# Attention probabilities: the fourth head of each group turned by VectorE and DMAs instead of TensorE

## The chip, the cores and the metric

One core of a Trainium2 chip. The time is device microseconds of one execution; lower is better. "Span" is the time from the first to the last instruction of one profiled execution.

## The reference

Two layers over x of 8 batches x 512 tokens x 512 features, in float32. The first is a graph attention in which each of 16 heads looks at 20 tokens, in two directions. The second, which the change touches, is a conditioned self-attention:

```python
h   = gamma(w) * layernorm(x) + beta(w)          # gamma, beta from the condition, per batch
q, k, v = split(h @ Wqkv.T + bqkv)               # 16 heads of 32
att = softmax(q @ k.T) / sqrt(512)               # [512 x 512] per batch and head
out = (att @ v).reshape(512, 512) @ Wp.T + bp
h1  = out + x
x   = gamma(w) * layernorm(h1) + beta(w) + h1
```

## The kernel before, in words

The first layer fills the first 400 us of the profile and leaves its result in DRAM (`mid`). The second layer is a loop over 128 **steps** (L1060 and after), in an order written out by hand for every engine. A step is one batch `b`, one group `g` of four heads and one block `c` of 128 queries; a batch has 16 steps, numbered by `at`. In the last batch the order of groups and blocks is exchanged.

In step n the kernel does, on TensorE in this order: the scores of step n+1 (four heads, each on its own 32 rows of the array, into two PSUM tiles of two banks); in steps 1 to 4 a **turn**, four transposes of the next batch's normalized tokens; in even steps the product of the probabilities with the values for the two steps before (`weigh`, L953), each head on its own 32 columns of the array, 16 products of 128 columns per step; then the transposes of this step's probabilities, head by head (`turn_probs`, L946, four 128x128 transposes a head), with a **job** after the second head and another after the third. A transposed head goes from PSUM to SBUF by a copy on ScalarE, that of the fourth head (outside the last batch) by VectorE. A float32 product is issued as two matmuls.

VectorE takes the maxima of the scores (`tops`, L931), ScalarE the exponentials with their sums (`exps`, L936), VectorE the reciprocals and GpSimd the scaling (`normalize`, L944), all one step ahead. When a group's four blocks are done, ScalarE adds the value bias and moves the group from PSUM to `AO` (`outputs`, L984).

The jobs of a batch are 32 slots, two per step (`JOBS`): the projections q, k, v of the next batch and the output projection. Both are made of seven products of half size, from sums and differences of quarters. For the output projection GpSimd makes those of the heads' outputs (`output_sums`, L775, at the steps of `OUTPUT_SUMS_AT`), and products 1, 6 and 7 are added to the residual by GpSimd (`add_gathered`, L823, at the end of the step that made them). Jobs `("output", 1, i)` are those of the batch before, `late` ones belong to the batch itself. Four more blocks of finishing per batch (`FINISH`: statistics, norm on VectorE, L879 and L880, sums on GpSimd, L883 and L884, a store) run in steps 5 to 8. Jobs and transposes share three PSUM banks.

All loads and stores of this layer are issued on SyncE's queue. `XQ[b]` holds a batch's input: fetched once, two batches ahead, normalized, and kept until it becomes the residual.

Of the kernel before, what the change touches and what calls it, by code (L numbers as in the profile page):

```python
# [9 lines left out]
F32 = mybir.dt.float32  # L10
BF16 = mybir.dt.bfloat16
I32 = mybir.dt.int32
AF = mybir.ActivationFunctionType
# [31 lines left out]
def graph_then_self_attention(ctx: ExitStack, tc: tile.TileContext, x, x_t, near, near_t, labels, w_self_t, wq, wk_t,  # L45
# [3 lines left out]
    def blocks(ap):  # L49
        return ap.rearrange("(c p) f -> p c f", p=P)  # L50
# [37 lines left out]
    XQ, Z, HT, Q, K, V, AO, GATE, STATS, PAIRS = {}, {}, {}, {}, {}, {}, {}, {}, {}, {}  # L88
# [11 lines left out]
    def fetch(b):  # L100
        XQ[b] = xp.tile([P, C, F], F32, tag="x", name=f"xq_{b}")
        nc.sync.dma_start(XQ[b], blocks(mid[b]))

    def norm_stats(b, c, src=None):
        statistics((src or XQ[b])[:, c, :], f"{b}_{c}")

    def norm(b, c, src=None):
        if c == 0:
            Z[b] = turned.tile([P, C, F], F32, tag="turned", name=f"z_{b}")
        mv = STATS[f"{b}_{c}"]  # L110
        nc.vector.tensor_scalar(Z[b][:, c, :], (src or XQ[b])[:, c, :], mv[:, 0:1], mv[:, 1:2], ALU.subtract, ALU.mult)
# [62 lines left out]
    with ExitStack() as l0:  # L174
# [452 lines left out]
        for n, (b, c) in enumerate(slots):  # L627
# [77 lines left out]
            if n in (23, 28):  # L705
                fetch((n - 23) // 5)
# [14 lines left out]
    gp = ctx.enter_context(tc.tile_pool(name="gp", bufs=1, reuse_waits="tile"))  # L721
    op = ctx.enter_context(tc.tile_pool(name="op", bufs=2, reuse_waits="tile"))
    ep = ctx.enter_context(tc.tile_pool(name="ep", bufs=8, reuse_waits="tile"))
    tp = ctx.enter_context(tc.tile_pool(name="tp", bufs=8, reuse_waits="tile"))
# [128 lines left out]
    def load_gate(b):  # L853
        pool, tag, shape = (turned, "turned", [P, C, F]) if b == B - 1 else (gp, "gate", [P, 2, F])
        GATE[b] = pool.tile(shape, F32, tag=tag, name=f"gate_{b}")[:, 0:2, :]
        nc.sync.dma_start(GATE[b], gates[b].partition_broadcast(P))
# [88 lines left out]

    def turn_probs(n, j, copy):  # L946
        pt = bank(f"pt1_{n}_{j}")
        for k in range(C):
            nc.tensor.transpose(pt[:, k * P:(k + 1) * P], E[n][j][:, k * P:(k + 1) * P], ident)  # L949
        et = ET[n, j] = tp.tile([P, C, P], F32, tag="et", name=f"et_{n}_{j}")  # L950
        copy(et, pt.rearrange("p (k n) -> p k n", k=C))  # L951

    def weigh(n):  # L953
        b, g, c = steps[n]
        last = b == B - 1
        if n + 1 == len(steps):
            PAO[b, g] = bank(f"pao_{b}_{g}_{c}")
        elif c == 0 or last:
            PAO[b, g] = ps_a.tile([P, 512], F32, tag="pao", name=f"pao_{b}_{g}_{c}")
        at = slice(c * P, (c + 1) * P)  # L960
        for k in range(C):
            for j in range(4):
                h = 4 * g + j
                nc.tensor.matmul(PAO[b, g][DH * j:DH * (j + 1), at], V[b][:, k, DH * h:DH * (h + 1)],  # L964
                                 ET[n, j][:, k, :], start=(k == 0), stop=(k == C - 1))

    def outputs(n):

        b, g, c = steps[n]
        last = b == B - 1  # L970
        at = slice(c * P, (c + 1) * P)
        if c == (0 if last else C - 1):
            if not last:
                if g % 2 == 0:
                    AO["pair", b, g // 2] = aop.tile([P, 2, N], F32, tag="ao", name=f"ao_{b}_pair_{g // 2}")
                AO[b, g] = AO["pair", b, g // 2][:, g % 2, :]
            else:
                if g == 0:
                    AO[b] = feat.tile([P, C, N], F32, tag="feat", name=f"ao_{b}")
                AO[b, g] = AO[b][:, g, :]  # L980
        if last:
            nc.scalar.activation(AO[b, g][:, at], PAO[b, g][:, at], AF.Identity, bias=bv[:, g:g + 1])
        elif c == C - 1:
            nc.scalar.activation(AO[b, g], PAO[b, g], AF.Identity, bias=bv[:, g:g + 1])  # L984


    def made(i, *ns):
        return [("product", i, n) for n in ns]
# [10 lines left out]
    for b in range(1, B - 1):  # L999
        JOBS[b] = (late[:1] + [None] + late[1:] + [("output", 1, n) for n in (2, 3, 6, 7, 4)] + made(v, 1) + [None]  # L1000
                   + made(v, 2, 6, 5, 3, 7, 4) + made(q, 1, 2, 6, 5) + made(k, 1) + [None] + made(k, 2, 6) + made(q, 3) + [None] + end)
# [9 lines left out]
    for b in range(1, B):  # L1011
        for block, first, second in (((b - 1, 0), 5, 6), ((b - 1, 1), 5, 6), ((b - 1, 2), 6, 8), ((b - 1, 3), 7, 8)) if b < B - 1 else (
# [7 lines left out]
    OUTPUT_SUMS_AT = {1: (1, 1), 2: (1, 2), 3: (1, 3), 10: (0, 0)}  # L1020
# [26 lines left out]
    with tc.manual_schedule():  # L1047
# [4 lines left out]
        fetch(2)  # L1052
# [17 lines left out]
        for n, (b, g, c) in enumerate(steps):  # L1070
# [12 lines left out]
            if last and at > 0:  # L1083
                if at > 1:
                    weigh(n - 2)
                    outputs(n - 2)
            elif n > 0 and n % 2 == 0:
                weigh(n - 2)
                weigh(n - 1)
# [20 lines left out]
            if n > 0 and n % 4 == 0 and (not last or at == 0):  # L1110
                outputs(n - 1)
# [20 lines left out]
            turn_probs(n, 3, nc.vector.tensor_copy)  # L1132
# [6 lines left out]

            if at == 0 and 0 < b < B - 1:  # L1140
                load_gate(b - 1)
            if at == 8 and b > 0 and b + 2 < B:
                fetch(b + 2)
# [64 lines left out]
```

## Time and profile before

| | |
|---|---|
| time, median of 3 runs | 1317.49 us (1315.29 to 1318.03) |
| span of the profiled execution (its own time is not given apart) | 1313.7 us |
| busy share of the span | PE 99%, VectorE 74%, GpSimd 64%, ScalarE 54% |
| DMA, mean busy share of its engines from 400 us on | 4 to 8% in windows of 100 us |
| one batch (637.07 to 752.60) | 115.5 us: TensorE 115.4 busy, VectorE 86.5, GpSimd 79.9, ScalarE 74.2 |
| granted TensorE clock | 1.00 in every window of 100 us up to 1200, 0.98 in the last |

In the profile's lines PE is TensorE's matmuls and PEld its weight loads, DVE is VectorE, ACT ScalarE, POOL GpSimd, SP SyncE. `pt` is a bank with transposed probabilities, `et` its copy, `e` the probabilities, `s` the scores, `pao` the product with the values, `pst` and `psp` the products of the projections and of the output projection. A timeline line gives start and length in us, the engine, the line of the kernel, the operation, what it writes and reads, how many instructions, and in brackets the idle time before it with what ended it. A group's line gives its count, its busy time in us and the mean of one in ns, then the idle time before it. Matmuls overlap, so the distance between two starts tells more than a length.

### The profile page before, as it was taken

What the parts mean: (1) busy time and instruction counts of PE and PEld (TensorE: products, weight loads), DVE (VectorE), ACT (ScalarE), POOL (GpSimd) and SP (SyncE); (2) the same over time, 40 slices, a digit from 0 to 9 for tenths busy, and PEclk for the clock granted to TensorE, in tenths of its full rate; (3) what the DMA queues carried; (4) which work ended last, traced back from release to release, by engine and by line L of the source; (5) the groups of instructions that cost most, each with busy time, mean ns of one, the idle gap of its engine ahead of it and who ended that gap; (6) DMA issues with size and microseconds to landing.
All of it is one profiled execution on the core that took longest, in us unless ns stands there. A gap on an engine that the chain in (4) does not pass through costs nothing.

```text
span 1313.7 us, 29713 instructions
## 1 busy us (share of the span) xinstructions
PE 1295.4 (99%) x11347; PEld 988.2 (75%) x11347; DVE 974.7 (74%) x1775; ACT 710.1 (54%) x1740; POOL 842.1 (64%) x905
## 2 busy tenths in 40 slices
PE   9999999999999999999999999999999999999997
PEld 6568887777765687777777777777777777777775
DVE  4479887888746678587677859767775976776886
ACT  2333233223225566766666676675666666666664
POOL 0067775677653546677578667747856775775776
PEclk9999999999999999999999999999999999999999
DMA  9533553253221000001002000100200010010010
GB/s 344 180 108 115 179 194 104 96 180 95 92 80 57 1 1 2 2 17 66 1 1 81 1 2 17 66 2 2 81 2 1 18 66 1 2 50 1 10 42 33
DMA packets 46491, 78.65 MB, mean 60 GB/s; under 512 B 9680, under 2 KB 14224, under 8 KB 46352
## 3 DMA queue, kind: packets, MB, share of 16 engines
q1 hardware_dynamic: 45920, 76.22, 17.0%
q8 instruction: 91, 1.49, 0.5%
q10 hardware_dynamic: 432, 0.55, 0.1%
q14 instruction: 48, 0.39, 0.1%
HBM read 59.27 MB, written 17.49 MB: 58 GB/s over the span
## 4 chain that ended last, share of the span: by engine, by line
PE 87%; DVE 8%; POOL 2%; issue 1%; ACT 1%; DMA 0%; POOLq 0%; DVEq 0%; ACTq 0%
PE pst L793 19%; PE pt L949 17%; PE s L924 10%; PE pss L532 8%; PE pao L964 8%; PE psp L836 6%; PE psf_p L359 4%; PE psf L312 2%; PE po L576 2%; PE pqk L138 2%; DVE top L931 2%; PE pz L124 1%; PE ptw L564 1%; PE pw L501 1%; PE pq L482 1%
## 5 line engine op out<-in xcount | busy, mean ns | idle before, releaser
L944 POOL TENSOR_SCALAR e<-e,den 128x512 f32<-128x512 f32 x511 | 366.8, 718 | 262.4 <-DVE den L941 168.5
L936 ACT ACTIVATE e<-s,top 128x512 f32<-128x512 f32 x512 | 348.9, 699 | 131.4 <-DVE top L931 131.2
L931 DVE TENSOR_REDUCE top<-s 128x2 f32<-128x1024 f32 x256 | 301.2, 1218 | 18.5 <-PE s L924 17.1
L949 PEld LDWEIGHTS pt<-ident,e 128*128 128x128 f32 x2048 | 234.5, 141 | 82.5 <-POOL e L944 25.9
L949 PE MATMUL pt<-ident,e 128*128 128x128 f32 x2048 | 289.7, 276 | 3.4 <-ACT et L951 1.3
L951 ACT COPY et<-pt 128x512 f32<-128x512 f32 x369 | 209.6, 597 | 101.1 <-PE pt L949 100.5
L924 PE MATMUL s<-k_pair,q_pair 32*128 32x512 f32 x992 | 143.8, 640 | 0.0
L532 PE MATMUL pss<-kq,sf 128*128 128x320 f32 x512 | 142.9, 432 | 0.0
L964 PEld LDWEIGHTS pao<-et,v 128*32 128x32 f32 x4096 | 107.5, 110 | 44.4 <-issue 44.4
L964 PE MATMUL pao<-et,v 128*32 128x128 f32 x4096 | 126.5, 274 | 0.0
L532 PEld LDWEIGHTS pss<-kq,sf 128*128 128x128 f32 x512 | 94.9, 190 | 36.1 <-ACT kq L489 0.3
L936 ACT ACTIVATION_READ_ACCUMULATOR e<-s,top 128x1 f32 x512 | 109.4, 214 | 0.0
L951 DVE COPY et<-pt 128x512 f32<-128x512 f32 x143 | 96.4, 674 | 3.4 <-PE pt L949 2.8
L538 POOL TENSOR_TENSOR t<-t,mask 128x640 f32<-128x640 f32 x32 | 49.5, 1547 | 65.6 <-DVE t L536 65.6
L558 POOL TENSOR_TENSOR t<-t,den 128x640 f32<-128x640 f32 x32 | 40.7, 1273 | 54.9 <-DVE den L557 54.3
L553 ACT ACTIVATE t<-t 128x640 f32<-128x640 f32 x32 | 23.6, 738 | 91.5 <-POOL t L550 91.5
L550 POOL TENSOR_TENSOR t<-t,top 128x640 f32<-128x640 f32 x32 | 47.4, 1480 | 38.9 <-DVE top L549 38.9
L126 ACT ACTIVATE ht<-pz,gates_t 128x512 f32<-128x512 f32 x32 | 24.7, 778 | 64.2 <-PE pz L124 64.2
L924 PEld LDWEIGHTS s<-k_pair,q_pair 32*128 32x128 f32 x992 | 41.2, 182 | 20.8 <-issue 17.4
L566 ACT COPY wt<-ptw 128x640 f32<-128x640 f32 x32 | 22.2, 694 | 61.2 <-PE ptw L564 61.1
L851 DVE TENSOR_TENSOR xq<-psp,xq 128x512 f32<-128x512 f32 x30 | 20.2, 689 | 45.9 <-PE psp L836 40.7
L793 PE MATMUL pst<-t,w 128*128 128x256 f32 x224 | 53.7, 383 | 0.0
(272 smaller groups left out, 2286.4 us busy)
## 6 DMA issues: line engine op xcount, KB each, us to landing
x<-in_x SPq DMA_DIRECT2D x8, 1024.0 KB
mid<-x SPq DMA_DIRECT2D x32, 256.0 KB
xq<-mid SPq DMA_DIRECT2D x8, 1024.0 KB
out<-o SPq DMA_DIRECT2D x31, 256.0 KB
vt<-in_x_t SPq DMA_DIRECT2D x7, 1024.0 KB
labels<-in_labels SPq DMA_DIRECT2D x16, 440.0 KB
wq<-in_wq SPq DMA_DIRECT2D x4, 1024.0 KB
gate<-gates SPq DMA_DIRECT2D x8, 512.0 KB
```

The source lines that it names most:

```text
L359: nc.tensor.matmul(o[:, m, :], a[:, k, m * P:(m + 1) * P], t[:, k, :], start=(k == 0), stop=(k == 1))
L532: nc.tensor.matmul(o, SF[b][:, k, cut], KQ[b][:, k, on], start=(k == 0), stop=(k == C - 1))
L538: nc.gpsimd.tensor_tensor(t, t, MASK[b][:, c, None].to_broadcast([P, H, D2]), ALU.mult)
L793: nc.tensor.matmul(out[:, m, :], fixed[:, k, m * P:(m + 1) * P], moving[:, k, :], start=(k == 0), stop=(k == 1))
L836: nc.tensor.matmul(out[:, m, :], t[:, k, m * P:(m + 1) * P], a[:, k, :], start=(k == 0), stop=(k == 1))
L924: nc.tensor.matmul(S[n][j // 2][:, j % 2, :], Q[b, g][on, c * P:(c + 1) * P], K[b, g][on, :], start=True, stop=True)
L931: nc.vector.tensor_reduce(TOP[n][:, 2 * pair:2 * pair + 2], S[n][pair], AX.X, ALU.max, negate=True)
L936: nc.scalar.activation(e, S[n][pair][:, j % 2, :], AF.Exp, bias=TOP[n][:, j:j + 1], accum_out=DEN[n][:, j:j + 1])
L944: engine.tensor_scalar(E[n][j], E[n][j], DEN[n][:, j:j + 1], att_scale, ALU.mult, ALU.mult)
L949: nc.tensor.transpose(pt[:, k * P:(k + 1) * P], E[n][j][:, k * P:(k + 1) * P], ident)
L951: copy(et, pt.rearrange("p (k n) -> p k n", k=C))
L964: nc.tensor.matmul(PAO[b, g][DH * j:DH * (j + 1), at], V[b][:, k, DH * h:DH * (h + 1)], ET[n, j][:, k, :], start=(k == 0), stop=(k == C - 1))
```

## The change

In the first seven batches the fourth head of each step is no longer transposed by TensorE. VectorE transposes it in squares of 32x32 (`turn_blocks`), into a tile that holds two steps. After every second step 16 DMAs on SyncE's queue (`gather`) move these squares to where a full transpose would have them, each 32 partitions by 4 runs of 64 numbers a partition. The product with the values takes two steps at once, 256 columns (`weigh_two`); the fourth head's is made one pair of steps after that of the other three. So a group's outputs are taken out of PSUM in two parts: rows 0 to 95 as before, rows 96 to 127 two steps later. `pao` becomes one tile for nearly all of the layer, and the transposed first three heads live in one tile of two steps.

Around this, the differences of outputs, the output jobs and the finishing of a batch move later. The gathered head takes one of the three large buffers of `xp`, so a batch's input is loaded twice: as `xn` for its normalization (step 10, two batches ahead) and again as `xq` for the residual (step 0 of its own batch). The gate vectors of a batch share the `turned` buffers and are loaded at step 2 instead of 0.

```diff
-    def fetch(b):
-        XQ[b] = xp.tile([P, C, F], F32, tag="x", name=f"xq_{b}")
-        nc.sync.dma_start(XQ[b], blocks(mid[b]))
+    def fetch(b, name="xq"):
+        t = xp.tile([P, C, F], F32, tag="x", name=f"{name}_{b}")
+        nc.sync.dma_start(t, blocks(mid[b]))
+        (XQ if name == "xq" else XN)[b] = t
...
-    tp = ctx.enter_context(tc.tile_pool(name="tp", bufs=8, reuse_waits="tile"))
+    tp = ctx.enter_context(tc.tile_pool(name="tp", bufs=1, reuse_waits="tile"))
+    bp = ctx.enter_context(tc.tile_pool(name="bp", bufs=2, reuse_waits="tile"))
...
     def load_gate(b):
-        pool, tag, shape = (turned, "turned", [P, C, F]) if b == B - 1 else (gp, "gate", [P, 2, F])
-        GATE[b] = pool.tile(shape, F32, tag=tag, name=f"gate_{b}")[:, 0:2, :]
+        GATE[b] = turned.tile([P, C, F], F32, tag="turned", name=f"gate_{b}")[:, 0:2, :]
         nc.sync.dma_start(GATE[b], gates[b].partition_broadcast(P))
...
+    BY_BLOCK = 3
+    ALONE = 16 * (B - 1)
+    turned_et = tp.tile([P, 2, BY_BLOCK, C, P], F32, name="turned_et")
+    gathered = xp.tile([P, C, F], F32, tag="x", name="gathered").rearrange(
+        "p k (i r c q) -> p i k r c q", i=2, r=4, c=2)
+    pao = ps_a.tile([P, 512], F32, tag="pao", name="pao")
...
-        et = ET[n, j] = tp.tile([P, C, P], F32, tag="et", name=f"et_{n}_{j}")
+        if j < BY_BLOCK:
+            et = turned_et[:, n % 2, j]
+        else:
+            et = bp.tile([P, C, P], F32, tag="blocks", name=f"et_{n}_{j}")
+        ET[n, j] = et
         copy(et, pt.rearrange("p (k n) -> p k n", k=C))
+
+    def turn_blocks(n):
+
+        if n % 2 == 0:
+            BLOCKS[n // 2] = bp.tile([P, 4 * C, 2, DH], F32, tag="blocks", name=f"blocks_{n // 2}")
+        nc.vector.transpose(BLOCKS[n // 2][:, :, n % 2, :], E[n][BY_BLOCK].rearrange("p (k q) -> p k q", q=DH))
+
+    def gather(m):
+
+        by_chunk = BLOCKS[m].rearrange("p (k s) c q -> p k s c q", s=4)
+        for r in range(4):
+            for s in range(4):
+                nc.sync.dma_start(gathered[DH * s:DH * (s + 1), m % 2, :, r], by_chunk[DH * r:DH * (r + 1), :, s])
...
-            PAO[b, g] = ps_a.tile([P, 512], F32, tag="pao", name=f"pao_{b}_{g}_{c}")
+        else:
+            PAO[b, g] = pao
...
-    def outputs(n):
+    def weigh_two(m):
+
+        for k in range(C):
+            for j in range(4):
+                n = 2 * (m if j < BY_BLOCK else m - 1)
+                if not 0 <= n < ALONE:
+                    continue
+                b, g, c = steps[n]
+                h = 4 * g + j
+                moving = turned_et[:, :, j, k, :] if j < BY_BLOCK else gathered[:, m % 2 ^ 1, k].rearrange("p r c q -> p c r q")
+                nc.tensor.matmul(pao[DH * j:DH * (j + 1), c * P:(c + 2) * P], V[b][:, k, DH * h:DH * (h + 1)],
+                                 moving, start=(k == 0), stop=(k == C - 1))
...
         elif c == C - 1:
-            nc.scalar.activation(AO[b, g], PAO[b, g], AF.Identity, bias=bv[:, g:g + 1])
+            nc.scalar.activation(AO[b, g][heads, :], pao[heads, :], AF.Identity, bias=bv[heads, g:g + 1])
...
     for b in range(1, B - 1):
-        JOBS[b] = (late[:1] + [None] + late[1:] + [("output", 1, n) for n in (2, 3, 6, 7, 4)] + made(v, 1) + [None]
-                   + made(v, 2, 6, 5, 3, 7, 4) + made(q, 1, 2, 6, 5) + made(k, 1) + [None] + made(k, 2, 6) + made(q, 3) + [None] + end)
+        JOBS[b] = (late[:1] + [None] + late[1:] + [None] + [("output", 1, n) for n in (2, 3)] + made(v, 1)
+                   + [("output", 1, n) for n in (6, 7)] + made(v, 2) + [("output", 1, 4)]
+                   + made(v, 6, 5, 3, 7, 4) + made(q, 1, 2, 6, 5) + made(k, 1) + [None] + made(k, 2, 6) + made(q, 3) + [None] + end)
...
-        for block, first, second in (((b - 1, 0), 5, 6), ((b - 1, 1), 5, 6), ((b - 1, 2), 6, 8), ((b - 1, 3), 7, 8)) if b < B - 1 else (
...
-    OUTPUT_SUMS_AT = {1: (1, 1), 2: (1, 2), 3: (1, 3), 10: (0, 0)}
+    OUTPUT_SUMS_AT = {3: (1, 1), 4: (1, 2), 5: (1, 3), 11: (0, 0)}
...
+                else:
+                    weigh_two(n // 2)
+                    outputs(n - 2, slice(DH * BY_BLOCK, P))
             elif n > 0 and n % 2 == 0:
-                weigh(n - 2)
-                weigh(n - 1)
+                weigh_two(n // 2 - 1)
...
             if n > 0 and n % 4 == 0 and (not last or at == 0):
-                outputs(n - 1)
+                outputs(n - 1, slice(0, DH * BY_BLOCK))
+            elif n > 4 and n % 4 == 2 and not last:
+                outputs(n - 3, slice(DH * BY_BLOCK, P))
+            if not last:
+                turn_blocks(n)
...
-            turn_probs(n, 3, nc.vector.tensor_copy)
+            if last:
+                turn_probs(n, 3, nc.vector.tensor_copy)
+            elif n % 2:
+                gather(n // 2)
...
+            if at == 2 and 0 < b < B - 1:
+                load_gate(b - 1)
             if at == 0 and 0 < b < B - 1:
-                load_gate(b - 1)
-            if at == 8 and b > 0 and b + 2 < B:
-                fetch(b + 2)
+                fetch(b)
+            if at == 10 and b + 1 < B:
+                if b + 2 < B:
+                    fetch(b + 2, "xn")
+                else:
+                    fetch(b + 1)
```

After the change the pools `bp` (squares of two pairs, or the fourth head's copy in the last batch) and `tp` (one tile) stand where `tp` had eight buffers before, and `norm_stats` and `norm` read `XN[b]`.

## The prediction

> **What bounds the kernel now.** I read the page first: its rows in 40 slices, then the chain that ended last, then the costliest groups.
>
> ```profile
> PEclk9999999999999999999999999999999999999999
> ...
> PE 87%; DVE 8%; POOL 2%; issue 1%; ACT 1%; DMA 0%; POOLq 0%; DVEq 0%; ACTq 0%
> PE pst L793 19%; PE pt L949 17%; PE s L924 10%; PE pss L532 8%; PE pao L964 8%; PE psp L836 6%; PE psf_p L359 4%; PE psf L312 2%; PE po L576 2%; PE pqk L138 2%; DVE top L931 2%; PE pz L124 1%; PE ptw L564 1%; PE pw L501 1%; PE pq L482 1%
> ...
> L949 PE MATMUL pt<-ident,e 128*128 128x128 f32 x2048 | 289.7, 276 | 3.4 <-ACT et L951 1.3
> ```
>
> TensorE is the chain for 87%, at full clock. The transposes of the probabilities (pt) are 17%: 223 us for 2048, 0.109 each. Their idle time is 3.4 us in all, so any transpose taken out shortens the chain, unless something else comes due. Next I read TensorE's timeline over an odd step and the start of an even one; what counts is the distance between starts.
>
> ```profile
> 804.26 1.09 PE L949 MATMUL pt<-ident,e 128*128 128x128 f32 x8
> 805.19 1.89 PE L793 MATMUL pst<-w,t 128*128 128x256 f32 x8
> 806.92 0.60 PE L949 MATMUL pt<-ident,e 128*128 128x128 f32 x4
> ...
> 809.08 0.60 PE L949 MATMUL pt<-ident,e 128*128 128x128 f32 x4
> 809.61 1.14 PE L924 MATMUL s<-k_pair,q_pair 32*128 32x512 f32 x8
> 810.68 1.96 PE L964 MATMUL pao<-et,v 128*32 128x128 f32 x64
> 812.57 1.09 PE L949 MATMUL pt<-ident,e 128*128 128x128 f32 x8
> ```
>
> Scores take 1.07, two heads' transposes 0.93, a projection product 1.73 (two per step, or fewer), one head's transposes 0.43 (before a product; 0.53 before scores), the values' product of two steps 1.89. An odd step is 6.42, an even one 8.31. Nothing waits. But at the start of a batch the other queues run close behind, as the timeline of all engines shows there (step 2 begins at 650.84, step 3 at 659.74, step 4 at 666.86):
>
> ```profile
> 655.32 1.89 PE L836 MATMUL psp<-s,ao_pair 128*128 128x256 f32 x8
> ...
> 657.34 0.22 ACT L936 ACTIVATION_READ_ACCUMULATOR e<-s,top 128x1 f32 x1
> ...
> 663.13 1.28 POOL L775 TENSOR_TENSOR ao_pair<-ao_pair,to 128x512 f32<-128x512 f32 x1
> ...
> 664.60 1.89 PE L836 MATMUL psp<-w,ao_pair 128*128 128x256 f32 x8
> ...
> 669.02 2.53 POOL L823 TENSOR_TENSOR xq<-y,xq 128x512 f32<-128x512 f32 x2
> ```
>
> In step 2 TensorE reaches its first job 4.4 us into the step, while ScalarE ends that step's exponentials 6.7 in. In step 3 GpSimd's last difference of outputs (L775) ends at 664.41, just when output product 4 wants it, and the two residual adds of product 7 come only after it. Last, busy time by engine in steps 5 to 8 (674.03 to 703.70):
>
> ```profile
> sum 29.67, PE 29.67 PEld 23.32 DVE 26.77 ACT 18.23 POOL 22.36; mean PE 7.42 PEld 5.83 DVE 6.69 ACT 4.56 POOL 5.59
> ```
>
> VectorE has 2.9 us to spare there in 29.7.
>
> **The change, part by part.** Everything is in us; the span is 1313.7, 3.8 below the median of 1317.49, and I carry differences over to the median.
>
> *Transposes out.* 112 steps lose one group of four: 112 x 0.43 = 48 (at 0.53: 59). I take -48.
>
> *Values' product.* Half as many instructions of 256 columns. A product's 8 of 256 columns need 1.73, 0.216 each; 32 on four column strips side by side are 32 x 0.216 / 4 = 1.73 against 1.89 now. That is at most 0.16 x 56 = 9 gained; the head read in runs of 32 could as well lose 9. I take -5.
>
> *VectorE.* A copy out of PSUM (0.67, L951) goes, a 32x32 transpose of 128x512 comes. The nearest rows are 0.54 (SBUF to SBUF, L879) and 1.22 (L931, twice the elements); I take 0.65, since it moves as many elements as the copy. The load stays, the place changes: the copy ran beside the next scores, the transpose stands behind the maxima (2.36) and ahead of the add that empties the first job's bank. In a plain step the maxima end at +3.5, the transpose at 4.2, the job at 3.9: nothing. At 1.22 the three fullest steps of six batches (below) would pay 0.57 x 18 = 10.
> [...]
>
> *Gather.* 16 issues per pair on SyncE. The issue row of vo, the small strided loads of the first layer, is the nearest:
>
> ```profile
> L519 SPq DMA_DIRECT2D vo<-vo_d x160: 265/331/1322, 53.7 to 360.1; - x160
> ```
>
> Twenty of them took 8.29 in a row (timeline of SP from 53.74), so 16 take 5.3 to 6.6. Landing is bounded by a load of 1 MB, 4.4 from its issue at 331.93 to the end of its traffic; I take 2 of 0 to 4.4. They start 4.2 into the odd step, and the product after next wants them 1.8 + 7.9 + 6.0 + 1.1 = 16.8 later: at least 5.8 to spare. On SP they queue behind output stores that wait for GpSimd (to about +5 of a step) and behind 1 MB loads, seven more of them now. I cost them at nothing; without the cover it is 56 times the lateness.
>
> *ScalarE* gains 28 activations of 0.72, hidden except in step 2 below.
>
> *Batch starts (b = 1 to 6).* This is where I expect the gain to go.
> Step 1 has only one job now. TensorE's own work shrinks to 1.07 + 0.49 (a turn) + 0.93 + 1.73 + 0.43 = 4.65, while its exponentials, behind four ScalarE evictions, now end 6.1 in (649.77 against 643.65) and hold the score banks. The second half of the next scores waits: 1.0, and 0.3 in the same way after step 0.
> Step 2: output product 2 now sits in the first job slot and reads head 3 of the last group, whose activation is issued in this very step after all four exponentials: 6.7 + 0.72 = 7.4 against 4.4. Wait 3.0.
> Step 4: product 7 wants a difference issued in that step. GpSimd first has the normalization (now from +1.1, since the job that VectorE empties before it ends with the step: 0.2 + 0.7 + 0.15; 1.48 long), one residual add (1.27), then the difference (1.28): done at 5.1 against 4.4. Wait 0.8.
> Step 5, odd: product 4 in the first slot wants the last difference. Ahead of it on GpSimd are 1.1 + 1.48, both residual adds of product 7 (2.53) and itself (1.28): 6.4 against 2.0. Wait 4.4.
> Together 9.5 per batch, 57 over six. Nothing else can run on TensorE meanwhile, as its order is fixed.
> The granted clock is 1.00 in every 100 us window but the last, so no row here prices a pause of 4.4 us.
> [...]
>
> *Steps 6 to 9.* Finishing moves on a step, so both blocks' norms (2.46) and two blocks' statistics (2.0) fall into step 7, odd: with maxima 2.36, transpose 0.65, three adds 2.0 and reciprocals 0.3 VectorE has 9.8 to do in a step of 6.0. In the four steps it has 27.4 (26.77, less two single adds, plus a single and a double) against 27.7 of TensorE (two plain pairs, 29.46, less 4 x 0.43). Step 8 gives back some 1.8 of the excess of 3.8; the rest delays maxima, exponentials and banks. Bounds 0 and 6 per batch; I take 3, 18 over six.
>
> *Elsewhere.* Steps 10 and 12 have one job and wait for normalization already (1.06 and 1.24 instead of 0.93 in the transposes after them); shorter by 0.43, they wait about that much more: 1 per batch, 6 in all. Entering the last batch head 3 alone runs on one strip: 8 x 0.216 = 1.7.
>
> Sum: -48 - 5 + 57 + 18 + 6 + 2 = +30. Forecast 1317.5 + 30, about 1347.
>
> **Rivals.**
> *The gain stays (faster).* Batch starts and steps 6 to 9 keep pace, because orders that I read as late turn out early enough. For: the other engines average 54 to 74% of the span. Against: the waits above are order in the queues, not load. Pure, 1317.5 - 48 - 5 + 2 = 1267. It decides if the waits per batch stay under 51 / 6 = 8.5.
> *The gathered head comes late.* If the product waited for the gather just issued (its halves lie interleaved in one tile) it would stand from +1.1 of the even step until 4.2 + 6.6 + 2 = 12.8 after the odd step's start, 6.0 long: 5.7 a pair, 320 over 56, some 1590 with the rest. Against: reads and writes touch different halves.
> *The pair's product gains nothing or loses.* 1.89 to 2.05 a pair: 1352 to 1361, inside my range.
>
> **Chances.** Forecast (waits eat the gain) 0.70, its own range 1318 to 1375; gain stays 0.22, spread from 1267 to 1320; late gather 0.05; something else, slower, 0.03. About 0.2% (2.6 us) can be told from no change. Slower by more: most of the 0.70 and the last two, 0.76; faster: 0.20; within: 0.04. To hold 8 in 10 the range reaches into the faster case: 1290 to 1375; its top is the forecast with all of 6 in steps 6 to 9 (+18) and a transpose of 1.22 (+10).
>
> **What would show it.** pt with 1600 matmuls; a new wait of TensorE on ao_pair L984 near 3 in step 2 and on GpSimd's L775 near 4.4 in step 5, six times each; VectorE full in steps 7 and 8; plain pairs of steps down from 14.73 to about 13.8. If TensorE's share stays at 99% and every batch shrinks by 7, I am wrong at the batch starts; if it waits on DMA, wrong on the gather.

## The result and the profile after

The changed kernel takes 1417.1 us (median of 4 runs, 1416.6 to 1422.1), the kernel before 1317.6 beside it: a ratio of 1.0765, 95% interval 1.0746 to 1.0783. That is +99.5 us, where the forecast had +30 and the range ended at 1375. The profiled execution took 1422.07 with a span of 1420.0, 106 over that of before; all of the working below is made between the two spans.

The page of the changed kernel, with the chain by engine and by line, then three groups (busy us, mean ns | idle us before, what ended it):

```profile
PE 65%; DVE 12%; POOL 9%; issue 4%; ACT 4%; SPq 3%; DMA 3%; POOLq 0%; DVEq 0%; ACTq 0%
PE pst L794 11%; PE pt L957 9%; PE pss L533 7%; PE s L924 7%; PE psp L837 6%; PE pao L1001 5%; PE psf_p L360 4%; SPq L976 3%; POOL e L944 3%; PE psf L313 2%; DMA xn<-mid 2%; ACT e L936 2%; PE pqk L139 2%; PE po L577 2%; DVE top L931 2%
...
L957 PE MATMUL pt<-ident,e 128*128 128x128 f32 x1600 | 235.6, 285 | 54.7 <-POOL e L944 46.4
...
L969 DVE STREAM_TRANSPOSE blocks<-e 128x512 f32<-128x512 f32 x112 | 78.9, 704 | 7.6 <-DMA gathered<-blocks 4.1
L837 PE MATMUL psp<-w,ao_pair 128*128 128x256 f32 x144 | 48.1, 485 | 39.1 <-POOL ao_pair L776 24.7
```

TensorE has lost the chain: 87% of it before, 65% now. The 448 transposes are gone, but those that are left had 3.4 us of idle time ahead of them before and have 54.7 now, 46.4 of it for GpSimd's scaling (L944), and the output products wait 39.1. The waits of the second layer from 420 to 1300 us (engine, tile, line <- what it waited for: us in total, times, longest):

```profile
PE pt L957 <- POOL e L944: 45.6, 13, 6.6
DVE o L879 <- DMA out<-o: 42.0, 6, 7.7
...
PE psp L837 <- POOL ao_pair L776: 27.9, 12, 4.1
...
PE psp L837 <- ACT ao_pair L1021: 14.4, 6, 2.4
```

The two waits on `ao_pair` were forecast. The one on `out<-o` was not: in each of six batches VectorE stands still for 7 us until an output store has landed. TensorE's timeline in the third batch shows what each wait cost (start, length; in brackets the idle time before):

```profile
671.60 2.60 PE L837 MATMUL psp<-w,ao_pair 128*128 128x256 f32 x6 [2.40 <-ACT ao_pair L1021]
...
688.79 1.99 PE L837 MATMUL psp<-s,ao_pair 128*128 128x256 f32 x8 [0.54 <-POOL ao_pair L776]
...
699.16 3.68 PE L837 MATMUL psp<-w,ao_pair 128*128 128x256 f32 x8 [4.11 <-POOL ao_pair L776]
...
735.53 1.97 PE L957 MATMUL pt<-ident,e 128*128 128x128 f32 x8 [5.48 <-POOL e L944]
737.30 3.35 PE L794 MATMUL pst<-t,s 128*128 128x256 f32 x8
```

These are steps 2, 4, 5 and 9. A product of eight such matmuls took 1.89 before. After the pause of 4.11 it takes 3.68; after the one of 5.48 eight transposes take 1.97 instead of 1.09 and the product behind them 3.35. The four microseconds after the pause of step 5, as a window (length, busy us of PE, PEld, DVE, ACT, POOL, then the granted clock, the DMA share and GB/s):

```profile
699.10:703.10 4.00, 3.94 (x12) 3.12 (x13) 0.15 (x1) 0.00 (x0) 1.23 (x2) 0.57 0.33 54
```

The clock is 0.57 there, 0.95 over the whole batch, and 1.00 over the first batch, which has no such pause. So each of these long pauses is paid once as a pause and again as slow work, 1.8 us in step 5. The pause of 2.40 in step 2 does the same in five of the six batches: in the 5.4 us after it the third batch has a clock of 0.68. In the fourth batch the same pause is followed by a clock of 1.00.

Where the store comes from is in the timeline of all engines in steps 7 to 9:

```profile
719.46 10.26 SPq L976 DMA_DIRECT2D gathered<-blocks  x16
...
726.38 1.28 POOL L884 TENSOR_TENSOR o<-o,xq 128x512 f32<-128x512 f32 x1
...
729.84 11.10 SPq L885 DMA_DIRECT2D out<-o  x3
...
732.15 0.55 DVE L879 TENSOR_SCALAR o<-xq,mv_h 128x512 f32<-128x512 f32 x1 [6.58 <-DMA out<-o]
```

The norm of finishing block 2, in step 8, wants one of the two output buffers that blocks 0 and 1 filled in step 7. Block 0's sum on GpSimd ends at 727.66; its store is issued at 729.84, when SyncE is through with the pair's sixteen transfers. The norm stands ahead of the transpose and the maxima on VectorE, so reciprocals, scaling and TensorE follow it. The sixteen take 10.3 us:

```profile
L976 SPq DMA_DIRECT2D gathered<-blocks x896: 585/599/1920, 418.5 to 1316.4; - x180
```

That is 0.60 for one issue (minimum, median, maximum in ns), where vo's row had 0.33.

The step lengths, as distances between the starts of the scores, averaged over batches 1 to 6, show the two places (the batches' sums in the last column; "first" is batch 0):

```
                                                first  steps 0-5  6-9   10-15   sum
before                                          118.1     43.6   29.3   40.9   113.8
changed                                         111.4     53.1   38.1   40.3   131.6
before, finishing as in the changed kernel      118.1     43.6   35.6   40.9   120.1
before, one norm a step to step 10              118.1     43.6   29.8   43.5   116.9
changed, finishing as in the kernel before      111.4     53.2   29.2   43.5   125.9
changed, output products put off                111.4     40.7   38.0   40.4   119.1
changed, one norm a step                        111.4     52.6   28.9   43.3   124.8
changed, put off, finishing as before           111.4     40.7   33.7   43.7   118.1
changed, put off, one norm a step               111.4     40.7   32.6   43.0   116.3
the same, product 7 half a step earlier         111.4     40.7   31.2   43.7   115.6
```

In batch 0, which has neither output products nor a finishing of an earlier batch, the change brings 6.7 us. In the next six it costs 17.7 each, 106 in all. The kernels of the last three rows leave something out of a norm (see "Both put together").

### The profile page after: what moved, and what is told of

The parts are those of the page before. It is cut to its first block, busy times and chain, and to the rows that moved or that the text cites. A ratio compares the mean times of both kernels' runs of the same rounds, so it can differ in the third digit from the quotient of the medians.

```text
span 1420.0 us, 26473 instructions
## 1 busy us (share of the span) xinstructions
PE 1300.4 (92%) x9107; PEld 922.5 (65%) x9107; DVE 982.5 (69%) x1775; ACT 732.4 (52%) x1768; POOL 836.0 (59%) x905
## 4 chain that ended last, share of the span: by engine, by line
PE 65%; DVE 12%; POOL 9%; issue 4%; ACT 4%; SPq 3%; DMA 3%; POOLq 0%; DVEq 0%; ACTq 0%
PE pst L794 11%; PE pt L957 9%; PE pss L533 7%; PE s L924 7%; PE psp L837 6%; PE pao L1001 5%; PE psf_p L360 4%; SPq L976 3%; POOL e L944 3%; PE psf L313 2%; DMA xn<-mid 2%; ACT e L936 2%; PE pqk L139 2%; PE po L577 2%; DVE top L931 2%
## 5 line engine op out<-in xcount | busy, mean ns | idle before, releaser
L944 POOL TENSOR_SCALAR e<-e,den 128x512 f32<-128x512 f32 x511 | 361.8, 708 | 372.1 <-DVE den L941 304.7
L963 ACT COPY turned_et<-pt 128x512 f32<-128x512 f32 x369 | 207.7, 592 | 177.1 <-PE pt L957 176.6
L957 PE MATMUL pt<-ident,e 128*128 128x128 f32 x1600 | 235.6, 285 | 54.7 <-POOL e L944 46.4
L957 PEld LDWEIGHTS pt<-ident,e 128*128 128x128 f32 x1600 | 187.4, 145 | 138.9 <-POOL e L944 87.9
L924 PE MATMUL s<-k_pair,q_pair 32*128 32x512 f32 x992 | 155.3, 640 | 1.0 <-ACT e L936 1.0
L1001 PE MATMUL pao<-gathered,v 128*32 128x256 f32 x448 | 107.2, 382 | 2.4 <-DMA gathered<-blocks 2.4
L1001 PE MATMUL pao<-turned_et,v 128*32 128x256 f32 x1344 | 107.9, 382 | 0.0
L1001 PEld LDWEIGHTS pao<-turned_et,v 128*32 128x32 f32 x1344 | 49.9, 109 | 63.1 <-issue 34.2
L852 DVE TENSOR_TENSOR xq<-psp,xq 128x512 f32<-128x512 f32 x30 | 20.2, 689 | 93.2 <-PE psp L837 93.2
L969 DVE STREAM_TRANSPOSE blocks<-e 128x512 f32<-128x512 f32 x112 | 78.9, 704 | 7.6 <-DMA gathered<-blocks 4.1
L837 PE MATMUL psp<-w,ao_pair 128*128 128x256 f32 x144 | 48.1, 485 | 39.1 <-POOL ao_pair L776 24.7
L559 POOL TENSOR_TENSOR t<-t,den 128x640 f32<-128x640 f32 x32 | 40.7, 1273 | 56.3 <-DVE den L558 55.7
L794 PE MATMUL pst<-t,s 128*128 128x256 f32 x224 | 61.7, 425 | 1.6 <-ACT turned_et L963 1.6
```

Of the source, the lines that this page charges most:

```text
L794: nc.tensor.matmul(out[:, m, :], fixed[:, k, m * P:(m + 1) * P], moving[:, k, :], start=(k == 0), stop=(k == 1))
L837: nc.tensor.matmul(out[:, m, :], t[:, k, m * P:(m + 1) * P], a[:, k, :], start=(k == 0), stop=(k == 1))
L924: nc.tensor.matmul(S[n][j // 2][:, j % 2, :], Q[b, g][on, c * P:(c + 1) * P], K[b, g][on, :], start=True, stop=True)
L944: engine.tensor_scalar(E[n][j], E[n][j], DEN[n][:, j:j + 1], att_scale, ALU.mult, ALU.mult)
L969: nc.vector.transpose(BLOCKS[n // 2][:, :, n % 2, :], E[n][BY_BLOCK].rearrange("p (k q) -> p k q", q=DH))
L1001: nc.tensor.matmul(pao[DH * j:DH * (j + 1), c * P:(c + 2) * P], V[b][:, k, DH * h:DH * (h + 1)], moving, start=(k == 0), stop=(k == C - 1))
```

## The experiments

Theory A: the loss is not in what was added but in the order around it, that is in the place of the output products (steps 2 to 5) and of the finishing (steps 6 to 9). Rivals: the sixteen transfers on SP's queue are the cost, or VectorE's transpose makes it the bound.

**The later finishing order in the kernel before.** Only this part of the diff:

```diff
-  ((b-1, 0), 5, 6), ((b-1, 1), 5, 6), ((b-1, 2), 6, 8), ((b-1, 3), 7, 8)
+  ((b-1, 0), 6, 7), ((b-1, 1), 6, 7), ((b-1, 2), 7, 8), ((b-1, 3), 7, 9)
```

> Kernel before with only the changed kernel's finishing steps (6 and 7, 6 and 7, 7 and 8, 7 and 9 instead of 5 and 6, 5 and 6, 6 and 8, 7 and 8). No gather here. Theory A (two output buffers, reused one step later): VectorE waits for the stores about 4 a batch, the time rises by 15 to 40, to 1333 to 1357. Theory C (the stores are late only because SyncE's queue is full of gathers): within 4 of the kernel before.

Measured: 1352.1, a ratio of 1.0272 (1.0255 to 1.0288), +36 us, without a single transfer or transpose. The waits of that run have a line which the kernel before doesn't have:

```profile
DVE o L879 <- DMA out<-o: 25.1, 6, 5.3
```

Steps 6 to 9 go from 29.3 to 35.6, step 8 alone from 8.1 to 12.1. So this one part is slower by itself, and the new wait is the one for the output buffers: the old order puts two norms into step 6 and two into step 8, the new one two into step 7 and one into step 8.

**The finishing order put back in the changed kernel**, the same edit the other way round.

> The changed kernel with the finishing order of the kernel before (statistics in steps 5, 5, 6, 7, norms in 6, 6, 8, 8); nothing is left out. Theory D (the later order alone made steps 6 to 9 long; two norms in one step, then two in the step after next, leave each output buffer two steps): steps 8 and 9 fall from 9.99 + 14.24 to 8 + 6.5, with the waits of steps 2, 4 and 5 left: 8 to 10 us in each of six batches, 1355-1370 us. Theory H (with transposes and transfers added, VectorE and SP are too full for this work in any order): 1385 us or more.

Measured: 1387.2, 30 less than the changed kernel. Steps 6 to 9 fall from 38.1 to 29.2, as theory D has it, but steps 10 to 15 rise by 3.2, most of it in step 13, so that the time ends just inside theory H's range. SP's queue and VectorE show why:

```profile
732.78 8.33 SPq L976 DMA_DIRECT2D gathered<-blocks  x13
741.15 0.59 SPq L102 DMA_DIRECT2D xn<-mid  x1
...
747.17 0.69 DVE L93 BATCH_NORM_STATS2 st<-xn 128x6 f32<-128x512 f32 x1 [2.35 <-DMA xn<-mid]
```

The load `xn`, written at the end of step 10 (which ended at 734.7), is issued at 741.15, after the last of the sixteen, and VectorE waits for it in step 12. A wait taken out in step 9 lets the queues run up against the next one.

**The output products put off**: product 2 to the first half of step 3, product 7 to the first half of step 5, product 4 to that of step 6.

```diff
-  late[:1] + [None] + late[1:] + [None] + [("output", 1, n) for n in (2, 3)] + made(v, 1)
-  + [("output", 1, n) for n in (6, 7)] + made(v, 2) + [("output", 1, 4)] + made(v, 6, 5, 3, 7, 4) + ...
+  late[:1] + [None] + late[1:] + [None] * 2 + made(v, 1) + [("output", 1, n) for n in (2, 3, 6)]
+  + made(v, 2) + [("output", 1, 7)] + made(v, 6) + [("output", 1, 4)] + made(v, 5, 3, 7, 4) + ...
```

> Changed kernel with only the order of the jobs in a batch altered: output products 2, 3, 6, 7 and 4 move to slots 6, 7, 8, 10 and 12 (from 4, 5, 7, 8 and 10), one value product to slot 5, an empty slot to 4. Theory A (order of the queues at the batch start): the waits on ScalarE's activation (2.4) and on GpSimd's differences (0.5 and 4.1) and the slow clock after the last go; steps 0 to 5 fall by 9 to 11 a batch, the time by 45 to 65, to 1352 to 1372. Theory B (the wait only moves to the next thing that is due): less than 20 gained.

Measured: 1347.3, ratio 1.0231 (1.0216 to 1.0246), 70 less than the changed kernel. TensorE's waits on L1021 and L776 are gone and steps 0 to 5 take 40.7 instead of 53.1, with one job of 1.7 moved out of them. The other wait stands as it was, and steps 6 to 9 with it (38.0):

```profile
DVE o L879 <- DMA out<-o: 41.3, 6, 7.3
```

So the two losses are separate. In this kernel the statistics of blocks 0 and 1 still stand behind product 4 in step 6, so nothing is left out.

**The reuse of the buffers.** First the third block's norm one step later, in step 9 with the fourth:

```diff
-  ((b-1, 2), 7, 8), ((b-1, 3), 7, 9)
+  ((b-1, 2), 7, 9), ((b-1, 3), 8, 9)
```

> Changed kernel with the finishing of a batch's four blocks two by two, two steps apart (steps 7, 7, 9, 9 instead of 7, 7, 8, 9). Theory A (buffers: the norm of block 2 waits for the store of block 0, one step earlier, to free one of two output buffers): VectorE's wait on the stores (42 us in the profile) goes, step 9 falls from 14.2 to near 7, and the time falls by 40 to 55, to 1362 to 1377. Theory B (VectorE is simply overfull in steps 6 to 9, as predicted): the time falls by less than 15.

Measured: 1397.1, only 20 less. The wait falls from 42.0 to 6.8 and step 9 from 14.24 to 7.92, but step 11 rises from 6.45 to 10.74: GpSimd now has two blocks' sums in a row (four of 1.27, from 733.7 to 738.9) ahead of the scaling, and TensorE waits for that. Then one block a step, norms in 6, 7, 8 and 9:

```diff
-  ((b-1, 0), 6, 7), ((b-1, 1), 6, 7), ((b-1, 2), 7, 8), ((b-1, 3), 7, 9)
+  ((b-1, 0), 5, 6), ((b-1, 1), 6, 7), ((b-1, 2), 7, 8), ((b-1, 3), 8, 9)
```

> The changed kernel with its four finishing blocks normalised one in each of steps 6, 7, 8 and 9 (statistics in 5, 6, 7, 8) instead of two in step 7 and one each in steps 8 and 9, so that each of the two output buffers is used again two steps after; nothing is left out. Theory D (reuse of an output buffer one step after is what makes steps 8 and 9 long): the wait for the stored output falls below 5 us, step 9 falls from 14.24 to under 8 and step 8 from 9.99 to under 9.5, no other step rises by over 1: 7 to 9 us in each of six batches, 1360-1378 us. Theory E (GpSimd's two sums of 1.27 us a block, not the buffers, are what fills these steps): the wait moves on to steps 10 and 11, as where two blocks were put in step 9 (step 11 took 10.74), and no more than 25 us come back: 1392 us or more.

Measured: 1382.0, 35 less than the changed kernel, the reuse two steps apart:

```profile
DVE o L879 <- DMA out<-o: 3.9, 5, 1.3
```

Steps 6 to 9 take 28.9, below the 29.3 of before, but steps 10 to 15 rise by 3.0 (steps 10, 11 and 13 by about 1 each). Theory D is right on the place, and the time 4 us above its range.

**SP's queue.** Without the 896 transfers, so that the fourth head's product reads zeros:

```diff
-            elif n % 2:
-                gather(n // 2)
```

> Changed kernel without the 896 gathering DMAs: VectorE still transposes the squares, and the product of the fourth head reads a tile of zeros, so that head is left out of the result. Theory A: the output buffer is still reused a step after its store can be issued, so VectorE's wait falls by the 2 or so that the store stood behind gathers; time 1417 less 10 to 25. Theory C (SyncE's queue): the whole wait of steps 8 and 9 goes, time down by 45 or more, to 1372 or less.

Measured: 1386.2, 31 less, between the theories, with the wait for the stored output still at 26.2, about what the kernel before shows with this finishing order (25.1). So the buffers' reuse alone makes 26 of the 42 us, and the hold behind the transfers the other 16. Then the stores ahead of the transfers, by moving `gather` behind the sums in the odd step:

```diff
-            elif n % 2:
-                gather(n // 2)
...
             finish_parts("sums")
+            if not last and n % 2:
+                gather(n // 2)
```

> The changed kernel with a pair's sixteen transfers issued after the finishing blocks' sums and output stores of the same step instead of ahead of them; nothing is left out. Theory A1 (the output buffer comes free late because its store waits on SP's queue behind sixteen issues of 0.60 us): in the changed kernel block 0's sum ended at 727.66 and its store landed near 732.1 only because SP issued transfers to 729.72; ahead of them it lands near 730, so VectorE's wait for the stored output falls from 42 us to about 28 and the time by 12 to 25 us, to 1392-1405 us. Theory D (the buffer is late because the sums themselves come late, and the queue adds nothing that matters): within 6 us of 1417.

Measured: 1442.3, 25 more than the changed kernel. Its waits:

```profile
DVE st L93 <- DMA xn<-mid: 25.7, 5, 6.4
DVE o L879 <- DMA out<-o: 25.6, 6, 4.4
...
PE pao L1001 <- DMA gathered<-blocks: 20.4, 10, 3.5
```

The wait for the stores falls as theory A1 said, to 25.6, yet the time rises: now the transfers stand behind stores that wait for GpSimd, so the gathered head is late, and the load `xn` behind them later still. It is one queue, and what is first in it only chooses who waits. The same edit on top of the output products put off and one norm a step (the next run):

> The same two edits and the transfers of a pair issued after the output stores; nothing is left out. Theory D alone: with two steps between uses of an output buffer the order on SP's queue no longer matters, within 4 us of the kernel with the two edits. Theory A1: each store still held up to 10 us behind sixteen issues costs something, so 5 to 15 us less than the kernel with the two edits. Theory F (the transfers themselves become late when put behind the stores): more by over 4 us, with TensorE waiting for the gathered head.

Measured: 1371.4 against 1329.5 without it (next run): theory F, +42, with 24.5 us of TensorE waiting for the gathered head.

**Both put together**: output products put off, one norm a step, the two diffs above.

> The changed kernel with both edits: the output products put off as in the run of 1347.31 us, and one finishing block a step (norms in steps 6, 7, 8, 9); nothing is left out. Theory D: the two waits are in different steps and add up; the steps 8, 9 and 10, 31.8 us together in the run of 1347.31, fall to about 23 (7.85 + 6 + 7.6 + 1.5), 8 to 10 us in each of six batches: 1287-1300 us, below the kernel before by 1 to 2 per cent; the granted clock of the layer is 0.99 or more. Theory E: 1325 us or more. If the waits at the batch's start had only hidden the finishing work, it is above 1347.

Measured: 1329.5, ratio 1.0102 (1.0086 to 1.0118), 88 less than the changed kernel. The mean granted clock is back at 0.996. This is 30 us above theory D's range: steps 7 and 8 take 8.33 and 9.78. A window over one step 8 of 10.1 us shows VectorE (third busy time) full, at a clock of 1.00:

```profile
692.80:702.90 10.10, 8.55 (x71) 5.35 (x70) 10.00 (x16) 4.51 (x13) 6.33 (x8) 1.00 0.30 63
```

The expectation says that nothing is left out, but something is. Product 4 is added to blocks 0 and 1 by VectorE (L852). Put off, it comes in step 6, and the statistics (step 5) and the norm (step 6) of block 0 now stand ahead of it. VectorE's timeline in the third batch:

```profile
675.53 0.67 DVE L93 BATCH_NORM_STATS2 st_h<-xq 128x6 f32<-128x512 f32 x1
...
682.23 1.48 DVE L879 TENSOR_SCALAR o<-xq,mv_h 128x512 f32<-128x512 f32 x1 [1.89 <-POOL xq L824]
...
685.94 0.65 DVE L852 TENSOR_TENSOR xq<-psp,xq 128x512 f32<-128x512 f32 x1
```

So this kernel leaves product 4 out of block 0's norm, and product 7, added by GpSimd from 680.92 on, out of its statistics. The work is the same, but a kernel that leaves nothing out can't take this order. That holds for the run with all three edits above and for every later run with the products put off: for blocks 0 and 1 in the next one, for block 0's statistics alone where product 4 is in step 5. Their times show where queues collide; none is the time of a version that could be used.

The same jobs and products, but with the finishing order of the kernel before:

> The same with the output products put off as in the run of 1347.31 us; nothing is left out. Theory D: steps 0 to 5 as there (40.7 against 43.6 of the kernel before), steps 6 to 9 about 29 (29.5 in the kernel before, less 1.7, plus up to 3 for VectorE), the rest 0.45 a step lower: 4 to 6 us less than the kernel before in each of six batches, 7 in the first: 1278-1295 us, faster than before by 1.5 to 3 per cent. Theory H: 1325 us or more, as with one block a step.

Measured: 1341.9, ratio 1.0184 (1.0169 to 1.0198): theory H by the number, but not for its reason. Step 7 takes 11.87. The products that were put off bring their residual adds on GpSimd into steps 5 and 6, and VectorE's first norm waits for them:

```profile
DVE o L879 <- POOL xq L824: 13.2, 6, 2.2
```

That is 2.2 of the 5.7 us by which step 7 is longer than without the products put off; what the rest divides into wasn't taken apart. The old finishing order gives back 5.4 us here instead of 30, and only by leaving product 4 out of two blocks' norms.

**What is left of it.** Norms in 6, 7, 9 and 10:

```diff
-  ((b-1, 2), 7, 8), ((b-1, 3), 8, 9)
+  ((b-1, 2), 8, 9), ((b-1, 3), 9, 10)
```

> The changed kernel with the output products put off and the finishing blocks' norms in steps 6, 7, 9 and 10 (statistics 5, 6, 8, 9); nothing is left out. With the norms in 6, 7, 8, 9 it took 1329.5 us, step 7 took 8.33 and step 8 9.78, VectorE 8.23 of 8.33 and 9.68 of 9.78 busy. Theory V (VectorE is simply full in these two steps, so that a block moved out of step 8 takes its share with it): step 8 falls to about 8, step 9 and 10 rise by 0.5 to 1 each: 1320-1328 us. Theory G (the transfers on SP's queue hold the rest): within 4 us of 1329.5.

Measured: 1335.4 (1332.4 to 1339.9), above both theories. Step 8 falls to 8.68, but step 13 rises to 9.94. Norms in 6, 8, 9 and 10:

```diff
-  ((b-1, 1), 6, 7), ((b-1, 2), 7, 8), ((b-1, 3), 8, 9)
+  ((b-1, 1), 7, 8), ((b-1, 2), 8, 9), ((b-1, 3), 9, 10)
```

> The same with the norms in steps 6, 8, 9 and 10 (statistics 5, 7, 8, 9); nothing is left out. Theory V: step 7 falls from 8.33 to about 6, step 8 stays near 9, steps 9 and 10 rise by under 1.5 together: 1 to 2.5 us in each of six batches, 1313-1324 us, level with the kernel before or up to 0.6 per cent behind it. Theory G: within 4 us of 1329.5.

Measured: 1330.5 (1328.6 to 1335.0), theory G's number; step 7 rises to 8.86 although VectorE is busy for only 7.3 of it. In three batches it takes 8.1, in the other three 9.5 to 9.8. The mean granted clock of that execution is 0.986, against 0.996 with the norms in 6, 7, 8 and 9; in which steps it fell isn't shown. That kernel without its transfers:

> The kernel with the norms in steps 6, 8, 9 and 10 and the output products put off, without its 896 gathering transfers; left out is the gathering of the fourth head, whose product uses a buffer of zeros. Theory V (with stores two steps apart SP's queue has nothing urgent behind the transfers): within 6 us of the same kernel with them. Theory G: 15 to 30 us less, as where they were taken from the changed kernel as it is (1386 against 1417).

Measured: 1325.9 (1323.8 to 1330.1), 4.5 less: theory V, so the number before had another cause than the transfers. Where the same removal brought 31 before, it is nearly nothing now, which fits the reading that SP's queue cost that much because a wait hung on it. And the kernel before with the norms in 6, 8, 9 and 10:

```diff
-  ((b-1, 0), 5, 6), ((b-1, 1), 5, 6), ((b-1, 2), 6, 8), ((b-1, 3), 7, 8)
+  ((b-1, 0), 5, 6), ((b-1, 1), 7, 8), ((b-1, 2), 8, 9), ((b-1, 3), 9, 10)
```

> The kernel before with the norms in steps 6, 8, 9 and 10 (statistics 5, 7, 8, 9), so that a gain of that order would be seen on both sides; nothing is left out. Its steps 6 to 9 have no wait over 1.9 us to lose: theory V expects 0 to 2 us less in each batch, 1305-1318 us. Theory D2 (any move of the finishing work out of its own order costs it as much as it cost the changed one): 1325 us or more.

Measured: 1336.9, ratio 1.0163 (1.0146 to 1.0180): theory D2. The old kernel loses 21 us by the order that suits the changed one; its steps 10 to 15 rise by 2.6.

**Product by product.** Products 7 and 4 half a step earlier, on the kernel with the products put off and one norm a step:

```diff
-  + [("output", 1, n) for n in (2, 3, 6)] + made(v, 2) + [("output", 1, 7)] + made(v, 6) + [("output", 1, 4)]
+  + [("output", 1, n) for n in (2, 3, 6, 7)] + made(v, 2) + [("output", 1, 4)] + made(v, 6)
```

> The changed kernel with one finishing block a step (norms in 6, 7, 8, 9) and the output products put off by half as much: products 7 and 4 in the second halves of steps 4 and 5 rather than in steps 5 and 6; nothing is left out. With products in 5 and 6 it took 1329.5 us. Theory K (GpSimd's two sums behind product 7, then in step 6, made VectorE's first norm wait and step 7 take 8.33): step 7 falls to about 6.5 and step 5 rises by up to 1.5 (product 4 comes half a step nearer to its input): 0.5 to 2 us in each of six batches, 1315-1326 us. Theory V (VectorE's own load is the limit there): within 4 us of 1329.5.

Measured: 1338.1 (1336.3 to 1346.4), worse by 9. Step 7 falls to 5.99 as theory K had it, but product 4 is early again: TensorE waits 3.2 for L776 in each batch and step 5 takes 10.86. With the load `xn` a step earlier:

```diff
-            if at == 10 and b + 1 < B:
+            if at == (9 if 0 < b and b + 2 < B else 10) and b + 1 < B:
```

> The same with the load of the next batch's input issued at the end of step 9 instead of step 10, so that it does not stand on SP's queue where it did; nothing is left out. Theory Q (the load, held behind the transfers, makes the statistics in step 12 wait and step 13 long, 8.50 against 6.68 in the kernel before): step 13 falls to about 6.5-7, 1 to 2 us in each of six batches: 6 to 12 us less than the kernel beside it. Theory V: within 4 us of it.

Measured: 1343.8 (1337.7 to 1346.3), no gain. Then product 7 half a step earlier and product 4 in step 6:

```diff
-  + [("output", 1, n) for n in (2, 3, 6, 7)] + made(v, 2) + [("output", 1, 4)] + made(v, 6)
+  + [("output", 1, n) for n in (2, 3, 6, 7)] + made(v, 2, 6) + [("output", 1, 4)]
```

> The changed kernel with one finishing block a step (norms in 6, 7, 8, 9), output product 7 in the second half of step 4 and product 4 in the first half of step 6; nothing is left out. Theory K (the two waits come from the place of one product each): step 5 near 6, step 7 near 6.5, the others as in the two runs before it: about 4 us less than 118.5 in each of six batches, 1308-1318 us, level with the kernel before or up to 0.7 per cent faster. Theory V (VectorE and GpSimd are full over steps 5 to 8 together, so the work lost in one step stands in the next): 1325 us or more.

Measured: 1323.4 (1318.9 to 1328.0), ratio 1.0055 (1.0036 to 1.0075), between the theories: the lowest time of all, 94 less than the changed kernel and still 7 more than the kernel before, but with product 4 left out of block 0's norm. Steps 5 and 7 are at 5.99 each, but step 6 rises to 8.84. With `xn` a step earlier:

> The same with the next batch's input loaded at the end of step 9 instead of step 10. Theory Q (the load's place on SP's queue makes step 13 long): 3 to 8 us less than the kernel beside it, as step 13 fell by only 0.4 when this was tried with product 4 in step 5; otherwise within 4 us of it.

Measured: 1324.9 (1317.7 to 1329.6), the same; step 13 is no shorter (9.64). So the load's place in the queue isn't what makes step 13 long here; what does stays open.

In this kernel (1323.4) most norms of blocks 1 to 3 fall beside GpSimd's sums, and VectorE is slower there (the median of its 31 L880 is 1.64):

```profile
704.48 1.27 POOL L883 TENSOR_TENSOR xq<-xq,gate 128x512 f32<-128x512 f32 x1
704.53 1.51 DVE L879 TENSOR_SCALAR o<-xq,mv_h 128x512 f32<-128x512 f32 x1
...
705.83 1.34 POOL L884 TENSOR_TENSOR o<-o,xq 128x512 f32<-128x512 f32 x1
706.07 1.65 DVE L880 TENSOR_TENSOR o<-o,gate 128x512 f32<-128x512 f32 x1
```

Where GpSimd is idle these two take 0.54 and 0.69 (the changed kernel, from 716.33 on), so this block costs 1.9 us more of VectorE. No run shows why it is slower there. That this is what fills step 8 (9.76) is argued, not shown.

Not tried were more than two output buffers, a second queue for the transfers, and one norm a step in steps 7 to 10 with the products put off, an order in which every norm could stand behind product 4.

## Why the prediction was wrong

The direction and the mechanism at the batch starts were right. Point by point, in us per batch for batches 1 to 6 unless said otherwise:

- *Transposes out, 48 over 112 steps.* Right: 6.7 per undisturbed batch, 47 over seven; plain pairs take 13.84 (forecast 13.8), pt has 1600 matmuls.
- *Values' product, -5.* Wrong, small: from the scores to the transposes it takes 1.87 a pair now as against 1.89. The rival that the pair's product gains nothing held, inside a larger miss.
- *VectorE's transpose, 0.65.* 0.704. In plain steps it costs nothing, as said.
- *Gather, 5.3 to 6.6 for sixteen, costed at nothing.* Mis-sized, and looked at from one side only. At the median of 0.60 sixteen make 9.6; the timeline's rows of sixteen take 10.3 to 11.7. The gathered head was in time (TensorE waited for it once, 2.4, at 1318, on entering the last batch), so that rival is out. But the text asked what the transfers would wait for on the queue, never what would wait for the transfers: the output stores, and with them the norm. Taking the transfers out brought 31 us.
- *Batch starts, 9.5.* The waits are there, six times each, and close: 2.40 for 3.0 in step 2, 0.54 for 0.8 in step 4, 4.11 for 4.4 in step 5. Steps 0 to 5 should have risen by 9.5 - 6 x 0.43 - 0.3 = 6.6 and rose by 9.6. The missing 3.0 (18 over six) is in the main slow clock: 1.8 in step 5 and, as a mean of the six batches, 1.4 in step 2, while the three waits were 1.2 shorter together than forecast; the last 1.0 isn't assigned. No row of before prices what follows a pause, and the sum has no term for it; the run shows 3.68 - 1.89 = 1.8 after the pause of 4.11 in the third batch. Step 2 was slowed too, in five of six batches, after a pause of only 2.40.
- *Steps 6 to 9, 3 of 0 to 6.* The step that failed. By the text they change by 3 - 4 x 0.43 - 0.2 = +1.1; they changed by +8.8. So the term that was put at 3 came to 10.7, beyond its upper bound of 6. The 7.7 more in each of six batches are 46 of the 76 missed between the spans. The working added up VectorE's load and stopped there. The load was nearly right, and there was room: with the old finishing order the changed kernel, VectorE's transposes included, does these steps in 29.2. What it left out is a resource with two places. `op` has two buffers; an order that moves the norms "on a step" also changes the distance between two uses of one buffer from two steps to one, so that the store of block 0, its sum on GpSimd and SP's queue all come onto the path. The same edit costs the kernel before 36 us (25.1 of it as the wait itself), and the transfers on SP make it worse.
- *Elsewhere.* Forecast -1.9 in steps 10 to 15, measured -0.6: step 13 is 1.3 longer. 8 over six. The last few are in the first and the last batch and ahead of the layer.

So the loss divides into some 70 us for the place of the output products and 30 to 36 for the finishing order, each shown by a run that changes it alone. The two can't simply be added: with the products put off, a norm of block 0 in step 6 comes before product 4. The best kernel that leaves nothing out is the one with the products put off alone, 1347.3, or 31 more than the kernel before. What the change itself is worth with everything around it in its best order stays open. The kernels with both edits, down to 1323.4, were still 7 us or more above the kernel before, and they have it easier at one place, as block 0's norm doesn't wait for product 4.

## What to carry to other kernels

When a step of work moves in time, list the buffers that it cycles through and recount the distance between two uses; a pool of two whose uses come one step apart puts a store, its sums and its queue on the path. On a shared DMA queue ask both what the new transfers wait for and what waits for them, in the order of issue: turning that order round moved the wait and made it dearer (+25 and +42 us). When a product is put off, look for everything that reads its sum: here a norm was left standing ahead of it. And a pause of TensorE is to be priced with the slow work that can follow it, here 1.8 us on top of 4.1.

## What was new of the hardware

A transfer of 32 partitions by 4 runs between two SBUF tiles holds SyncE's queue for 0.60 us per issue (median of 896), almost twice the 0.33 of the first layer's strided loads (median of 160). TensorE's clock fell not only after the pauses of 4.11 and 5.48: after the same pause of 2.40 it was at 0.50 for 3.41 us in five of six batches and stayed at 1.00 in the fourth. In the changed kernel between 400 and 1300 us there are 17 such stretches, 11 of 3.41 us and 6 of 6.83, and all begin and end on one grid of 3.41. Each of the 17 comes after an interval of that grid in which TensorE was idle for 62% or more (by the trace's modelled ends), and no interval idle for up to 48% has one behind it. In the third batch the pause of 2.40 lies in one interval (668.56 to 671.97, TensorE busy for 1.01 of 3.41), and the clock of the next is 0.50; in the fourth it is divided between two (798.26 to 805.09, busy for 2.21 and 2.22), and the clock behind them stays at 1.00. So in this trace it matters where a pause lies on that grid. And VectorE's norm and product took 1.5 and 1.65 beside GpSimd's sums instead of 0.54 and 0.69; beside GpSimd's scaling (L944), in the kernel before from 698.83 on, they took 0.54 to 0.92 and 0.98.
